# ConvNeXt block and two-layer Mamba mixer in one launch: scan states kept in pairs, multiplied by C in place by GpSimd

## The chip, the core and the metric

The kernel runs on one core of a Trainium2 chip. The metric is device time in microseconds of one execution. The engines are called as in the profile: PE (TensorE, matmuls), PEld (its weight loads), DVE (VectorE), ACT (ScalarE), POOL (GpSimd) and SP (the engine that here only issues DMAs). Each executes its own queue in order and waits on semaphores of the others.

## The reference, cut to what matters

The input is x, 32 images of 96 channels of 56x56 in float32. Layer 0 is a ConvNeXt block, layer 1 two Mamba blocks, a pooled branch, a 1x1 fusion, a batch norm and a residual.

```python
# layer 0
h = depthwise_conv7x7(x) + conv_b                    # groups = 96
h = gelu(layernorm_over_channels(h) @ w1 + b1) @ w2 + b2
x = h * layer_scale + x
# layer 1: seq is x as (image, 3136 positions, 96); two blocks
xz = layernorm(seq) @ in_w                           # 96 -> 2 * 192
xs, z = split(xz)
xc = silu(causal_conv4(xs) + conv_b)
dbl = xc @ xproj_w                                   # 192 -> 6 + 16 + 16
delta = softplus(dbl[:6] @ dt_w + dt_b)
dA  = exp(delta[..., None] * A)                      # 192 channels x 16 states
dBx = delta[..., None] * B[:, None, :] * xc[..., None]
h[t] = dA[t] * h[t-1] + dBx[t]                       # along 3136 positions
y = (sum over states of h * C) + D * xc
seq = seq + (y * silu(z)) @ out_w
# then: fusion with a pooled vector, batch norm, + x
```

The recurrence over h, with 192 x 16 = 3072 rows of 3136 positions for each image and block, is the bulk of the work.

## The kernel before

**Tiling.** The positions of an image are cut into four chunks of CH = 784, each of two halves of HC = 392. A *stage* is one chunk of one image in one Mamba block: 32 x 4 x 2 = 256 stages, one after another, with the two blocks interleaved (line 852). In a stage the 3072 rows are 24 *steps* of 128 partitions: step r is block of 32 channels j = r // 4 (six of them) and state group g = r % 4 (four states for each of the 32 channels, so 128 rows). Each step is one scan of 128x784 on DVE.

**One step.** ACT computes dA with an exponential (`exps`, line 890) from delta spread over the partitions (tile `d4`, by DMA). For blocks j = 0, 1, 3, 4 the factor u = delta * xc is spread to 128 partitions by PE (`spread`, line 905) into a PSUM tile and DVE multiplies it by B (`times_b`, line 878), four times for each block. For blocks 2 and 5 (`POOLED`) POOL does that product in SBUF (`pooled`, line 915). DVE scans (line 938) into a ring of four tiles `h`; one operand is in PSUM, the other in SBUF (`in_psum` tells which). POOL multiplies h by C into a tile `da` (line 942). PE sums the four states of a channel with a 0/1 matrix (`add_up`, line 975, two matmuls of 32 output rows for each step, one for each half) into the PSUM tile `y` of two blocks, which begins with D * xc (line 969). DVE multiplies y by silu(z) (`gate`, line 956), three times in a stage. ACT keeps the last column of h as the start of the next chunk (`keep_state`, line 949), not in the last chunk of an image.

**PSUM.** Eight banks: three for projections (`ps0` to `ps2`), two wide tiles of two banks (`wide(0)` holds the spread u and some exponentials, `wide(1)` products and some exponentials), one for `y`.

**What sets the order.** Every engine's order is written out by hand (`manual_schedule`, line 1011). The loop at line 1021 goes over the steps: in each it emits the exponentials of one or two steps ahead, `keep_state` of the step before, the step's scan with its products, then the spread of the next block and the sums of the step LAG = 3 before. Everything else is cut into *pieces* with a slot, a number in steps relative to a stage: the projections and norms that prepare the next stage (`prep`, 24 steps ahead), the output projection of the last one (`post`), and, in the shade of these, the ConvNeXt block of the later images (`block0`) and the depthwise convolution of the last 20 images (`conv`, five images at a time, one channel pair in each of 192 stages, line 552: seven matmuls of 112x168 and seven of 112x112). A piece with slot 7.5 is emitted behind step 7.

**Buffers.** A tile name has a fixed number of buffers; the writer of a new tile waits until the last reader of an old one is done. Here `da` has 11, `h` 4 (the ring), `bc` (B and C of one group, 6272 bytes a partition) 8, `d4` 3, `u` 1.

Ahead of the stages lie the convolution of the first 12 images and the ConvNeXt block of the first; behind them a normalisation of the whole output from DRAM (lines 1069 to 1078).

Of the kernel before, what the change touches and what calls it, by code (L numbers as in the profile page):

```python
# [44 lines left out]
C = 96  # L45
# [16 lines left out]
def convnext_mamba_kernel(  # L62
# [211 lines left out]
    for i in range(2):  # L274
        d = {}
        lg, lb = column(ln_g[i], C, f"lg{i}"), column(ln_b[i], C, f"lb{i}")
        wz = const.tile([C + 1, 2 * DIN], F32, name=f"inw{i}", tag=f"inw{i}")
        norm_weights(wz, in_w[i], lg, lb)
        wx = const.tile([C + 1, 4, DIN], F32, name=f"wx{i}", tag=f"wx{i}")
        nc.gpsimd.dma_start(wx, taps[i].partition_broadcast(C + 1))  # L280
        for k in range(4):
            nc.vector.tensor_tensor(wx[:, k, :], wx[:, k, :], wz[:, 0:DIN], ALU.mult)
        d["wx"], d["wz"] = wx, wz[:, DIN : 2 * DIN]
# [60 lines left out]
    with ExitStack() as main:  # L344
# [7 lines left out]
        def work(shape, name, bufs):  # L352

            pool, n = (pre[0], 3) if pre else (wp, bufs)
            return pool.tile(shape, F32, name=name, tag=name, bufs=n)
# [42 lines left out]
        xins = {}  # L398

        def block0(b, c, s):  # L400
# [16 lines left out]
            def load_x():  # L417
                if s == 0:
                    xins[b, c] = work([C, CH], "xin", 1)
                    nc.sync.dma_start(xins[b, c], x[b, :, c * CH : (c + 1) * CH])  # L420
# [36 lines left out]
            def down():  # L457
                v["ps"] = psum(2)
                nc.tensor.matmul(
                    v["ps"][0:C, 0:HC], eye, xins[b, c][:, tok(s)], start=True, stop=False  # L460
# [7 lines left out]
            def residual():  # L468
                xs = xins[b, c][:, tok(s)]
                nc.scalar.activation(  # L470
                    xs, v["ps"][0:C, 0:HC], AF.Identity, bias=b2ls,
                    accum_out=batch_sums[b][:, k : k + 1],
                )
                if s == 1:
                    nc.sync.dma_start(x1_d[b][:, c * CH : (c + 1) * CH], xins.pop((b, c)))
# [6 lines left out]
            def pool():  # L482
                ps = psum(2)
# [4 lines left out]
            def fuse():  # L488
                ps = psum(2)
# [9 lines left out]
            last = [(21.5, total), (29.9, pool), (30.9, fuse)] if k == 2 * NCH - 1 else []  # L499
            return last + [  # L500
                (-6, load), (2, load_x), (11.3, center), (12.1, square), (12.4, mean),
                (12.8, root), (14.1, True, norm), (15.6, up), (15.9, gelu), (17.3, down),
                (18.3, residual),
# [28 lines left out]
        PARTS = (0, (NB + 1) // 2), ((NB + 1) // 2, NB)  # L532

        def conv(g, p):
# [11 lines left out]
            def tap(part, dw):  # L546
                first, last = PARTS[part]

                def piece():
                    if dw == 0:  # L550
                        v["ps"] = psum(2)
                    nc.tensor.matmul(  # L552
                        v["ps"][0:R2, 0 : (last - first) * W], v["band"][:, dw, :],
                        xpad[:, first:last, dw : dw + W], start=(dw == 0), stop=(dw == 6),
# [4 lines left out]
            def store(part):  # L559
                first, last = PARTS[part]  # L560
                n = (last - first) * W

                def piece():
                    t = wp.tile([R2, HC], F32, name="sq", tag="sq", bufs=3)
                    nc.scalar.activation(
                        t[:, 0:n], v["ps"][0:R2, 0:n], AF.Identity, bias=cb[:, p : p + 1]
                    )
                    nc.sync.dma_start(
                        conv_d[g][p * R2 : (p + 1) * R2, first * W : last * W], t[:, 0:n]
                    )  # L570

                return piece

            at = (7.7, 8.2, 8.6, 9.2, 9.6, 10.2, 10.4), (18.5, 18.6, 19.2, 20.2, 21.2, 21.3, 22.2)
            return [
                (-1, load), (11.05, store(0)), (22.9, store(1)),
                *[(at[part][dw], tap(part, dw)) for part in range(2) for dw in range(7)],
            ]


        POOLED = (2, 5)
        seqs = {}
# [4 lines left out]
        def prep(S):  # L587
# [28 lines left out]
            def norm():  # L616
                hn = v["hn"] = hns[i]
                if c == 0:
                    nc.vector.memset(hn[:, 0:3], 0.0)
# [88 lines left out]
            def product(lo, hi):  # L708
                def piece():
                    if lo == 0:  # L710
                        S.u = wp.tile([128, NQ, HC], F32, name="u", tag="u", bufs=1)
# [426 lines left out]
```

## Time and profile before

| what | value |
|---|---|
| median of 3 runs | 16957.93 us (16953.4 to 16958.45) |
| the profiled execution | 16951.94 us |
| its span, first to last instruction | 16950.2 us |
| busy: PE / DVE / ACT / POOL | 15327.0 / 15667.8 / 11444.5 / 15657.7 us |
| first POOL product of the stages' steady run | about 570 us after the start |
| last matmul | before 16600 us |

An engine is busy in the profile while at least one of its instructions runs. Instructions of an engine overlap a little at their ends, so the sum of durations is above the busy time, and a stretch of back-to-back instructions tells the cost of one better than its duration does. Matmul ends are modelled: a busy PE is not a PE at its limit. A wait is put down to the instruction that released it last.

### The profile page before, as it was taken

How to read it: one execution, taken by the hardware profiler on the slowest of the kernel's cores; microseconds unless marked ns; L12 is line 12 of the kernel's file. 1: busy time of each engine (PE TensorE's matmuls, PEld its weight loads, DVE VectorE, ACT ScalarE, POOL GpSimd, SP SyncE). 2: the span in 40 equal slices, each digit the busy share in tenths (PEclk: the TensorE clock that was granted, in tenths of full speed). 3: DMA queues.
4: the chain of work that ended last, by engine and by line, in shares of the span. 5: the costliest groups of instructions: out<-in, count | busy, mean ns of one | idle time of the engine just before them, and what ended most of it. 6: DMA issues, size and time to landing. Idle time of an engine off the chain costs nothing. (4 is left out here: it accounts for less than half of the span.)

```text
span 16950.2 us, 206740 instructions
## 1 busy us (share of the span) xinstructions
PE 15327.0 (90%) x69336; PEld 5507.9 (32%) x69336; DVE 15667.8 (92%) x12351; ACT 11444.5 (68%) x18723; POOL 15657.7 (92%) x8798
## 2 busy tenths in 40 slices
PE   8899999999999999999999999999998888888881
PEld 5333333333333333333333333333332222222220
DVE  8699999999999999999999999999999999999994
ACT  1577777777777777777777777677776777676653
POOL 1699999999999999999999999999999999999991
PEclk9899999999999999999999999999999999999985
DMA  4344444444444444444444444444443433433338
GB/s 113 109 139 142 142 135 140 139 142 141 135 142 140 142 135 140 142 141 137 138 141 141 142 134 141 140 143 137 137 142 131 133 126 129 134 132 133 125 121 280
DMA packets 1303109, 2362.11 MB, mean 139 GB/s; under 512 B 516398, under 2 KB 669242, under 8 KB 1302040
## 3 DMA queue, kind: packets, MB, share of 16 engines
q1 hardware_dynamic: 1292712, 2308.46, 42.0%
q10 hardware_dynamic: 7168, 38.54, 0.6%
q8 instruction: 546, 8.95, 0.2%
q14 instruction: 523, 4.28, 0.1%
q0 software_dynamic: 2160, 1.88, 0.1%
HBM read 1945.97 MB, written 402.41 MB: 139 GB/s over the span
## 5 line engine op out<-in xcount | busy, mean ns | idle before, releaser
L942 POOL TENSOR_TENSOR da<-h,bc 128x784 f32<-128x784 f32 x6144 | 11296.0, 1864 | 428.7 <-DVE h L938 356.3
L975 PE MATMUL y<-da,ssum 128*32 128x392 f32 x24576 | 5193.2, 547 | 232.7 <-POOL da L942 229.1
L890 ACT ACTIVATE w<-d,A 128x784 f32<-128x784 f32 x3072 | 2810.9, 916 | 2442.6 <-DVE h L938 2403.6
L938 DVE TENSOR_TENSOR_SCAN h<-w,st,da 128x784 f32<-128x784 f32 x2304 | 4120.7, 1831 | 267.6 <-ACT w L890 261.5
L938 DVE TENSOR_TENSOR_SCAN h<-da,st,w 128x784 f32<-128x784 f32 x2304 | 4176.3, 1834 | 3.6 <-ACT st L949 3.2
L915 POOL TENSOR_TENSOR da<-us,bc 128x784 f32<-128x784 f32 x2048 | 3811.8, 1861 | 0.0
L878 DVE TENSOR_TENSOR w<-w,bc 128x784 f32<-128x784 f32 x3072 | 2910.6, 978 | 325.6 <-PE w L905 257.4
L890 ACT ACTIVATE da<-d,A 128x784 f32<-128x784 f32 x3072 | 2834.6, 939 | 19.0 <-DMA d<-dd 16.0
L633 PE MATMUL ps<-hn,wx 97*64 97x392 f32 x12288 | 2263.2, 503 | 11.0 <-DVE hn L621 11.0
L975 PEld LDWEIGHTS y<-da,ssum 128*32 128x32 f32 x24576 | 1079.4, 116 | 3366.9 <-issue 2015.7
L905 PE MATMUL w<-u,sel 64*128 64x392 f32 x4096 | 992.4, 560 | 555.8 <-DVE h L938 436.8
L938 DVE TENSOR_TENSOR_SCAN h<-w,da 128x784 f32<-128x784 f32 x768 | 1327.4, 1771 | 125.6 <-ACT w L890 118.0
L938 DVE TENSOR_TENSOR_SCAN h<-da,w 128x784 f32<-128x784 f32 x768 | 1345.4, 1773 | 0.0
L633 PEld LDWEIGHTS ps<-hn,wx 97*64 97x64 f32 x12288 | 797.5, 136 | 1422.4 <-issue 1113.2
L712 POOL TENSOR_TENSOR u<-dl,xc 128x784 f32<-128x784 f32 (+1 forms) x512 | 736.9, 1439 | 471.0 <-ACT dl L698 471.0
L552 PE MATMUL ps<-xpad,band 112*112 112x168 f32 (+1 forms) x5376 | 1086.6, 312 | 0.0
L552 PEld LDWEIGHTS ps<-xpad,band 112*112 112x112 f32 x5376 | 709.8, 175 | 1088.3 <-issue 972.7
L690 PE MATMUL ps<-dbl,dtw 6*64 6x392 f32 x3072 | 728.0, 536 | 310.9 <-ACT dbl L668 310.9
L878 DVE TENSOR_TENSOR da<-w,bc 128x784 f32<-128x784 f32 x1024 | 988.0, 965 | 1.0 <-DMA bc<-bd 1.0
L368 ACT ACT_TABLE_LOAD x759 | 973.8, 1283 | 14.2 <-PEq L1125 0.8
L377 ACT ACTIVATE sq<-ps 96x392 f32<-96x392 f32 x768 | 345.1, 490 | 759.9 <-PE ps L372 343.6
L969 PE MATMUL y<-xc,D 128*128 128x392 f32 x1536 | 790.3, 601 | 32.8 <-DVE z L956 32.8
(152 smaller groups left out, 14579.4 us busy)
## 6 DMA issues: line engine op xcount, KB each, us to landing
bc<-bd SPq DMA_DIRECT2D x2048, 392.0 KB, 6.5
d<-dd SPq DMA_DIRECT2D x1536, 392.0 KB, 3.6
us<-uu SPq DMA_DIRECT2D x512, 392.0 KB, 3.3
dd<-dl SPq DMA_DIRECT2D x512, 294.0 KB, 3.7
band<-band_d SPq DMA_DIRECT2D x192, 343.0 KB, 4.3
uu<-u SPq DMA_DIRECT2D x1024, 49.0 KB, 3.0
cv<-conv_d SPq DMA_DIRECT2D x256, 147.0 KB, 3.4
xin<-in_x SPq DMA_DIRECT2D x128, 294.0 KB, 3.9
```

Source lines behind the costliest of these rows:

```text
L368: nc.scalar.preload_act_table_set("natural_log_exp_and_others")
L552: nc.tensor.matmul(v["ps"][0:R2, 0 : (last - first) * W], v["band"][:, dw, :], xpad[:, first:last, dw : dw + W], start=(dw == 0), stop=(dw ...
L633: nc.tensor.matmul(v["x", q][rows(a), 0:HC], weights[:, k, 64 * q : 64 * q + 64], v["hn"][:, o : o + HC], start=(k == 0), stop=(k == last),)
L712: nc.gpsimd.tensor_tensor(S.u[:, lo:hi], v["dl"][:, lo:hi], S.xc[:, lo:hi], ALU.mult)
L878: nc.vector.tensor_tensor(halves(out), S.u4.rearrange("p (a b) -> p a b", a=2)[:, :, 0:HC], halves(S.bcs[g][:, 0, :]), ALU.mult,)
L890: nc.scalar.activation(e, S.d4[j], AF.Exp, scale=S.d["A"][:, j, g : g + 1])
L905: nc.tensor.matmul(S.u4[:, 512 * a : 512 * a + HC], sel[rows(a), j % 2, :], S.u[rows(a), j // 2, :], start=True, stop=True,)
L915: nc.gpsimd.tensor_tensor(product_tile(S, j, g), S.us[j], S.bcs[g][:, 0, :], ALU.mult)
L938: nc.vector.tensor_tensor_scan(ring[:, g, :], S.e.pop((j, g)), db, 0.0 if c == 0 else d["st"][:, j, g : g + 1], ALU.mult, ALU.add,)
L942: nc.gpsimd.tensor_tensor(da, ring[:, g, :], S.bcs[g][:, 1, :], ALU.mult)
L969: nc.tensor.matmul(S.y[:, 0:HC], S.d["D"][:, q, :], S.xc[:, q, :], start=True, stop=False)
L975: nc.tensor.matmul(S.y[r0 : r0 + 32, 0:HC], ssum, da[:, tok(a)], start=False, stop=(g == NG - 1),)
```

## The change

All of it is in the stages and their preparation.

1. **State pairs.** The scans of g = 0, 1 and of g = 2, 3 write the two halves of one SBUF tile `h` of 128 x 2 x 784 (7 buffers; `states`). The ring and the role of `da` as product tile go; `da` (now 4 buffers, NE) holds exponentials alone. The product of u and B of g = 3, and the pooled products, are written into the `h` tile, and the scan runs in place over them.
2. **h*C in place.** POOL multiplies a whole pair by C in one instruction of 128 x 2 x 784, in place. Where a next chunk follows, the instruction leaves out the last column (2 x 783); `keep_state` copies that column and multiplies it by C with two ACTIVATEs of 128x1.
3. **Pooled products** also go in pairs (two instructions for a block, with u broadcast over the pair), emitted at the slots in `AHEAD`, and **u** is one POOL instruction for all three q (128x1176) at slot 13.8, not one of 784 and one of 392.
4. **B and C** lie in tiles of their own, `bp` (3 buffers) and `cp` (4), each for two groups; the eight loads of a stage remain and two move to slots 15 and 17.9.
5. **State sums.** `add_up` takes the pairs of both blocks of a `y` at once, eight matmuls in a row to the four column tiles 0, 32, 64, 96, twice for each y, four steps behind.
6. **Spreads and gates** get fixed steps: spreads of blocks 0, 3 and 4 are emitted one step earlier than before (SPREADS), gates at steps 5, 13 and 20.
7. **Depthwise convolution in one part:** seven matmuls of 112x280 at steps 4 to 10, one store; none at steps 18 to 22.
8. **Slots** of the preparation are set anew; the input of the ConvNeXt block is loaded, and its result stored, by half chunks; half of the in_w weights is copied to a tile of its own and the other half freed after setup.

```diff
-            at = (7.7, 8.2, 8.6, 9.2, 9.6, 10.2, 10.4), (18.5, 18.6, 19.2, 20.2, 21.2, 21.3, 22.2)
+            at = (4.9, 6.1, 7.2, 8.6, 9.2, 9.6, 10.4)
+            return [(-1, load), (10.5, store), *[(at[dw], tap(dw)) for dw in range(7)]]
...
+        AHEAD = {(2, 0): -0.1, (2, 1): 4.4, (5, 0): 12.1, (5, 1): 16.9}
...
-            t = (-7.6, -7.5, -6.5, -6, 0, 0.1, 1, 2.3, 3.1, 3.4, 4)
+            t = (-4.5, -4.4, -5.3, -2.9, -4.2, -0.3, 0.8, 2.3, 2.9, 3.4, 4)
...
-        ring = wp.tile([128, NG, CH], F32, name="h", tag="h", bufs=1)
-        LAG = 3
-        LATE = (4, 12)
+        NE = 4
+        LAG = 4
+        LAG0 = 4
+        GATES = (5, 13, 20)
+        SPREADS = [(22, 0), (27, 1), (34, 3), (38, 4)]
+        WS = ((0, 3), (1, 2), (), ())
...
+        def states(S, j, h):
+            if (j, h) not in S.h:
+                S.h[j, h] = wp.tile([128, 2, CH], F32, name="h", tag="h", bufs=7)
+            return S.h[j, h]
...
-                nc.gpsimd.tensor_tensor(
-                    product_tile(S, j, g), S.us[j], S.bcs[g][:, 0, :], ALU.mult
-                )
+                nc.gpsimd.tensor_tensor(
+                    states(S, j, h), S.us[j].unsqueeze(1).broadcast_to([128, 2, CH]), S.bc[0, h],
+                    ALU.mult,
+                )
...
             nc.vector.tensor_tensor_scan(
-                ring[:, g, :], S.e.pop((j, g)), db, 0.0 if c == 0 else d["st"][:, j, g : g + 1],
-                ALU.mult, ALU.add,
+                h[:, g % 2, :], S.e.pop((j, g)), S.pb.pop((j, g), h[:, g % 2, :]),
+                0.0 if c == 0 else d["st"][:, j, g : g + 1], ALU.mult, ALU.add,
             )
-            nc.gpsimd.tensor_tensor(da, ring[:, g, :], S.bcs[g][:, 1, :], ALU.mult)
+            if g % 2 == 1:
+                hc = h[:, :, 0 : CH if c == NCH - 1 else CH - 1]
+                nc.gpsimd.tensor_tensor(hc, hc, S.bc[1, g // 2][:, :, 0 : hc.shape[2]], ALU.mult)
...
-                nc.scalar.copy(
-                    S.d["st"][:, j, g - 1 : g + 1].unsqueeze(2), ring[:, g - 1 : g + 1, CH - 1 : CH]
-                )
+                h, last = S.h[j, g // 2], slice(CH - 1, CH)
+                nc.scalar.copy(S.d["st"][:, j, g - 1 : g + 1].unsqueeze(2), h[:, :, last])
+                for k in range(2):
+                    nc.scalar.activation(
+                        h[:, k, last], h[:, k, last], AF.Identity,
+                        scale=S.bc[1, g // 2][:, k, last],
+                    )
...
-            for a in range(2):
-                r0 = 64 * a + 32 * (j % 2)
-                nc.tensor.matmul(
-                    S.y[r0 : r0 + 32, 0:HC], ssum, da[:, tok(a)],
-                    start=False, stop=(g == NG - 1),
-                )
+            hs = [S.h.pop((2 * q + k, half)) for k in range(2)]
+            for g in range(2):
+                for k in range(2):
+                    for a in range(2):
+                        r0 = 64 * a + 32 * k
+                        nc.tensor.matmul(
+                            S.y[r0 : r0 + 32, 0:HC], ssum, hs[k][:, g, tok(a)],
+                            start=False, stop=(half == 1 and g == 1),
+                        )
...
-                    if n % NG == NG - 1:
-                        spread(n + 1)
+                    for k, j in SPREADS:
+                        if n >= k - NSTEP and (n - k) % NSTEP == 0:
+                            spread(((n - k) // NSTEP + 1, j))
```

## The prediction

> **What bounds the kernel now.** I read the busy table first, then two stretches of the stages, then the waits, then single instructions. A measurement of this kernel can tell about 0.2%, 34 us, from no change.
>
> ```profile
> PE 15327.0 (90%) x69336; PEld 5507.9 (32%) x69336; DVE 15667.8 (92%) x12351; ACT 11444.5 (68%) x18723; POOL 15657.7 (92%) x8798
> ```
>
> Three engines seem equally full, so the whole span does not decide. The stretch 4000 to 12000 us has convolution pieces in every stage, 13000 to 16000 us none (the 192 pairs are used up). Columns: busy us and instructions of PE, PEld, DVE, ACT, POOL, then clock, DMA share and GB/s.
>
> ```profile
> 4000.00:12000.00 8000.00, 7541.04 (x34841) 2709.31 (x34839) 7587.62 (x5928) 5653.24 (x9335) 7801.02 (x4348) 0.96 0.43 140
> 13000.00:16000.00 3000.00, 2680.03 (x11776) 888.54 (x11773) 2853.86 (x2234) 2102.03 (x3417) 2934.66 (x1638) 0.93 0.40 130
> ```
>
> The scan line has 3070 instructions in the first and 1156 in the second. At 24 for each stage a stage takes 8000 x 24 / 3070 = 62.54 us with and 62.28 us without convolution. Per stage POOL is busy 60.98 us (60.92 without), DVE 59.32, ACT 44.2. POOL is 97.5% and 97.8% busy: it is the bound, DVE 1.7 us behind. DVE's waits in the two stretches, and the same for the second:
>
> ```profile
> DVE h L938 <- ACT w L890: 197.8, 135, 1.7
> DVE w L878 <- PE w L905: 151.0, 183, 1.1
> DVE z L956 <- PE y L975: 23.0, 44, 1.5
> ```
>
> ```profile
> DVE h L938 <- ACT w L890: 60.5, 49, 2.4
> DVE z L956 <- PE y L975: 58.2, 35, 4.0
> ```
>
> With convolution the waits are 2.9 us a stage, for exponentials and for the spread; without it the spread is never late, yet DVE waits 2.7 us, now for y, whose sums wait for POOL. The time stayed and only the name of the wait moved: DVE is held to POOL's pace. That is why I count POOL's instructions first.
>
> ```profile
> L942 POOL TENSOR_TENSOR da<-h,bc 128x784 f32<-128x784 f32 x6144 | 11296.0, 1864 | 428.7 <-DVE h L938 356.3 <-DVE hn L619 24.7 <-PE y L975 19.2
> L712 POOL TENSOR_TENSOR u<-dl,xc 128x784 f32<-128x784 f32 x256 | 473.8, 1851 | 471.0 <-ACT dl L698 471.0
> L712 POOL TENSOR_TENSOR u<-dl,xc 128x392 f32<-128x392 f32 x256 | 263.2, 1028 | 0.0
> ```
>
> ```profile
> 8013.76 10.94 POOL L942 TENSOR_TENSOR da<-h,bc 128x784 f32<-128x784 f32 x6
> ...
> 8028.31 1.02 POOL L712 TENSOR_TENSOR u<-dl,xc 128x392 f32<-128x392 f32 x1
> 8029.29 1.85 POOL L942 TENSOR_TENSOR da<-h,bc 128x784 f32<-128x784 f32 x1
> ```
>
> Here the reader sees what one POOL instruction costs in a row: six of 784 in 10.94 us, 1.82 each; one of 392 is followed after 0.98. So 2.14 ns for an element and 0.14 us for an instruction. From the durations (1851 and 1028) it is 2.10 ns and 0.205 us.
>
> And DVE's two regular waits of a stage, at its first product (step 0) and its fourth scan (step 3):
>
> ```profile
> 8018.26 0.98 DVE L878 TENSOR_TENSOR w<-w,bc 128x784 f32<-128x784 f32 x1 [0.78 <-PE w L905]
> ...
> 8028.70 1.79 DVE L938 TENSOR_TENSOR_SCAN h<-w,da 128x784 f32<-128x784 f32 x1 [1.63 <-ACT w L890]
> ```
>
> **What the Trainium skill says.** "GPSIMD Engine Reference", § 3.1 Elementwise: a two-input tensor_tensor of 2048 fp32 takes 4497 ns. My two numbers give 0.14 + 2048 x 2.14 = 4.52 us, so the line through 392 and 784 carries on to the 1568 elements of a pair, which no trace shows yet. "SBUF — State Buffer", § Who interferes with whom: a DVE instruction with two SBUF inputs blocks against a POOL instruction that reads SBUF, one with a single SBUF input does not. The trace agrees as far as it goes: scans with one operand in PSUM take 1831 and 1834 ns in the two arrangements while POOL is 97% busy. After the change each product and scan still has one of each, so I charge no contention. "TensorEngine Tiling (Array Packing)", § Key Properties: tiles of the array work in parallel; the sums now use two column tiles in turn (four matmuls in 0.85 us), after the change four.
>
> **The change, part by part, for a stage.**
>
> POOL. 24 products with C and 8 pooled ones become 12 and 4, u two to one: 17 instructions fewer, elements the same (the missing last column is 0.04 us). Saving 17 x 0.14 = 2.4 us by the rhythm, 3.5 us by the durations. I take 2.4: POOL 60.98 - 2.4 = 58.6 us. Unknown is what writing in place, two rows of 783 instead of one of 784, and the broadcast u cost. Ends: 57.5 us (3.5 saved); 61.3 us, if a pair costs 5% more than counted (16 x 0.17 = 2.7). A loss is not excluded.
>
> DVE. The same 24 scans, 16 products, three gates and the norms: 59.3 us. Scanning in place is the nearest to the form with `da` as input (1831 ns): 0. DVE becomes the bound, by 0.7 us.
>
> ACT. `keep_state` gains two ACTIVATEs of 128x1 for each of 12 pairs in three of four stages, 18 on average. The nearest row is the 96x1 negation, 195 ns; "ScalarE: Activation LUTs", § What ACT_TABLE_LOAD costs, has 186 ns plus 93 for a pointer operand, less 93 of overlap. So 18 x 0.19 = 3.4 us (5.0 at 0.28), less 0.25 for one convolution store: 47 to 49 of some 60 us. They hide in ACT's wait for DVE to free a wide tile (2403.6 us in the run, 9.4 a stage). Behind them are the exponentials; in a pooled block DVE takes 1.79 a step and ACT 0.86 for the exponential, 0.19 more a step on average. If that cover is gone, it is 0.4 us for each pair.
>
> PE. 48 sum matmuls in 12 groups of four, 0.85 each: 10.2 us. In six groups of eight, 5 us if four tiles work at once, 9 if not (eight two-tile projections take 1.54). Seven convolution matmuls of 280 columns, about 0.42 (between 331 ns for 168 and 451 for 336 columns, carried on), 2.9 us for 4.4. PE is not the bound; what counts is its order. The spread of block 0 stood behind convolution taps at 8015.55 and 8016.91 and started at 17.29; block 5's third scan had freed the tile at about 8015.7. It now comes a step earlier, without taps in front: the 0.8 us wait goes, and the like before block 3. The scan's wait at step 3 comes from ACT, which stood 1.58 us behind the convolution store at slot 22.9 (now 10.5) and 1.08 us for the third projection (slot 0.1, now -0.3). What is late next is POOL itself, or DVE has nothing to wait for.
>
> SP. Eight loads of B and C as before; four loads and four stores of half chunks more for an image, one convolution store less a stage. The load at slot 17.9 waits for DVE to leave `bp` at step 17; behind it are u's store and `d4`. The us tile is needed at step 23, some 15 us later, the two transfers take 3.0 + 3.3: 0. The smaller tiles at the start: 0, within 10 us.
>
> Latency. POOL starts a product only when two scans are done. The tightest sum, that of block 1 at PE step 9 behind scan 5, has 3 x 1.79 = 5.4 us for 3.5: hidden while POOL lags under 1.9 us.
>
> **The sum.** A bound engine in this coupling idles 1.56 us a stage with and 1.36 without convolution (62.54 - 60.98, 62.28 - 60.92). With DVE as the bound I take 1.4: 59.3 + 1.4 = 60.7 us. Saved 192 x 1.84 + 64 x 1.58 = 454 us. From the profiled execution, 16951.9 (its span of 16950.2 and 1.7 around it): 16497. The median stands 6 us higher: 16503, rounded 16500. The 957 us outside the stages are left as they are.
>
> **Rivals**, priced as 256 stages from a mean of 62.5 us.
> - *Nearly full DVE.* The two regular waits go and nothing follows: 59.5 to 60.1 us, 16196 to 16350. For it: both waits have named causes that are moved. Against: POOL has only 0.7 us to spare.
> - *POOL stays the bound*, since in-place pairs save less than counted or nothing: 59.9 to 60.9 busy plus 1.4, 61.3 to 62.3 us, 16657 to 16913, middle 16785. For it: the form is unseen. Against: the line of 392, 784 and 2048.
> - *Nothing gained*: DVE's waits are ACT's and PE's own, and stay near 3 us: 16924 to 16992. Against: the moving name of the wait above.
> - *Slower: seven `h` tiles.* At slot 16.9 POOL's product for block 5 needs an eighth tile; one comes free only when PE reads the pairs of blocks 2 and 3 at step 17, behind the ConvNeXt matmuls of slot 15.6. The product of slot 4.4 likewise hangs on the sums of step 3, behind the z projections. POOL waits in order, with the next products by C, so the sums and y, behind it. At 58.6 us busy it can lose 3.9 us a stage before a stage is as long as now, so it decides from about 2 us at each place; with 2.5, 63.6 us a stage, 17240. For it: PE already stands behind such work (520.6 us for dbl in the run). Against: PE gets freer.
>
> **Chances.** Forecast (60.1 to 61.3 us, 16350 to 16657) 0.50; nearly full DVE 0.16; POOL still the bound 0.18; nothing gained 0.04; slower 0.12. Range 16250 to 16880: it leaves out the slower and the equal case and 0.02 at each end. Faster 0.50 + 0.16 + 0.18 = 0.84, same 0.04, slower 0.12.
>
> **What would show it.** POOL pairs near 3.5 us and u near 2.65; POOL's busy time a stage under DVE's, which stays at 59.3; no wait of the first product for the spread; scans at 1.83. It is wrong if pairs take 3.65 or more, if POOL waits for PE at the pooled products, or if DVE's waits stay near 3 us a stage.

## The result, and the profile after

| | before | after |
|---|---|---|
| median | 16958.19 us (16953.4 to 16967.83, 4 runs) | 16698.44 us (16695.08 to 16705.25, 4 runs) |
| ratio, 95% interval | | 0.9847 (0.983 to 0.9864) |
| profiled span | 16950.2 us | 16693.4 us |
| mean granted TensorE clock | 0.943 | 0.871 |

The kernel became 1.5% faster, by 260 us; 458 us were forecast (16500). The time lies in the range given (16250 to 16880), but outside the band of the forecast itself (16350 to 16657). The busy table of the kernel after:

```profile
PE 13702.7 (82%) x66648; PEld 5300.0 (32%) x66648; DVE 15622.8 (94%) x12353; ACT 12429.3 (74%) x23139; POOL 15025.8 (90%) x4446
```

The groups of the changed instructions (pairs by C, pooled pairs, u, the last column):

```profile
L932 POOL TENSOR_TENSOR h<-h,cp 128x1566 f32<-128x1566 f32 (+1 forms) x3072 | 10753.6, 3523 | 408.2 <-DVE h L926 394.5
...
L909 POOL TENSOR_TENSOR h<-us,bp 128x1568 f32<-128x1568 f32 x1024 | 3608.9, 3524 | 265.8 <-PE y L975 161.7
...
L697 POOL TENSOR_TENSOR u<-dl,xc 128x1176 f32<-128x1176 f32 x256 | 684.3, 2673 | 598.2 <-ACT dl L685 469.8
...
L942 ACT ACTIVATE h<-h,cp 128x1 f32<-128x1 f32 x4608 | 1105.6, 287 | 102.1 <-ACT st L940 1.5
```

Every POOL duration is the forecast one: 3.52 us for a pair (3.5), 2.67 for u (2.65). The two stretches of the stages, after (columns as in the prediction):

```profile
4000.00:12000.00 8000.00, 6805.72 (x33497) 2632.73 (x33499) 7657.49 (x6003) 6215.57 (x11627) 7578.84 (x2202) 0.88 0.45 141
13000.00:16000.00 3000.00, 2445.55 (x12042) 881.02 (x12042) 2915.55 (x2290) 2341.71 (x4400) 2885.24 (x839) 0.87 0.42 134
```

They hold 3108 and 1182 scans, so a stage takes 8000 x 24 / 3108 = 61.78 us with convolution and 60.91 without; 60.7 was forecast for both. In the first stretch (129.5 stages) POOL is busy 58.5 us a stage, DVE 59.1, ACT 48.0: again the forecast numbers. What is not as forecast is DVE's idle time: 61.78 - 59.13 = 2.65 us a stage, and 1.7 without convolution, where the sum had 1.4. DVE's waits, first stretch and then second:

```profile
DVE h L926 <- ACT w L884: 275.5, 174, 3.6
...
DVE z L950 <- PE y L975: 0.3, 1, 0.3
```

```profile
DVE h L926 <- ACT w L884: 57.3, 52, 2.3
```

No wait for a spread is left and none for y; all that counts is one kind, scans that wait for an exponential. Adding up DVE's idle pieces over 0.1 us by the step that follows (stages 40 to 169 with convolution, 200 to 249 without, counted from 0) shows which scans. Stage lengths in this table are from the starts of the scans in the same stages:

| us a stage, with convolution | before | after |
|---|---|---|
| step 0, spread from PE | 0.79 | - |
| step 3, exponential from ACT | 1.47 | - |
| step 10, exponential | - | 0.50 |
| step 12, spread | 0.38 | - |
| step 19, exponential | - | 1.59 |
| step 20, y | 0.17 | - |
| all idle pieces | 3.03 | 2.46 |
| stage | 62.55 | 61.80 |
| *without convolution:* all idle pieces / stage | 2.83 / 62.35 | 1.49 / 60.82 |

The three waits that the prediction named are gone, and a new one at step 19 is larger than any of them. It is 0.85 us in stages without convolution, where the kernel before waited 1.20 us at step 3 and 1.26 at step 20. One instance in full, DVE first:

```profile
8085.94 3.57 DVE L926 TENSOR_TENSOR_SCAN h<-da,st,w 128x784 f32<-128x784 f32 x2
8091.54 1.85 DVE L926 TENSOR_TENSOR_SCAN h<-w,st,h 128x784 f32<-128x784 f32 x1 [2.03 <-ACT w L884]
```

The exponential that it waits for, on ACT:

```profile
8087.91 0.19 ACT L808 ACTIVATION_READ_ACCUMULATOR sq<-seq,neg 96x1 f32 x1
8090.02 0.58 ACT L469 ACTIVATE xin<-ps,b2ls 96x392 f32<-96x392 f32 x1 [1.92 <-PE ps L463]
8090.51 0.19 ACT L469 ACTIVATION_READ_ACCUMULATOR xin<-ps,b2ls 96x1 f32 x1
8090.60 0.90 ACT L884 ACTIVATE w<-d,A 128x784 f32<-128x784 f32 x1
```

ACT sat 1.92 us ready to compute the exponential, behind line 469 in its order: `residual`, the last step of the ConvNeXt block, which waited for matmuls. The change moved it from slot 18.3 to 17.6, that is, to ahead of this exponential. Why the matmuls were late, on PE (the trace shows each matmul of the program as two instructions, and the counts are of instructions):

```profile
8077.88 1.68 PE L899 MATMUL w<-u,sel 64*128 64x392 f32 x4 [3.49 <-DVE h L926]
8079.49 4.29 PE L443 MATMUL ps<-hz,w_sb 97*128 97x392 f32 x6
8083.57 1.51 PE L967 MATMUL y<-xc,D 128*128 128x392 f32 x2
8085.01 2.17 PE L975 MATMUL y<-h,ssum 128*32 128x392 f32 x16
8087.11 0.90 PE L459 MATMUL ps<-xin,eye 96*96 96x392 f32 x2
8087.85 2.14 PE L463 MATMUL ps<-gl,w_sb 128*96 128x392 f32 x6
```

PE stood 3.49 us before the spread of block 4 (step 14), the wide tile of which DVE had not yet freed. Then six instructions of line 443 (`up`, the first projection of the ConvNeXt block) took 4.29 us; those of line 463 (`down`, the second one), of as many columns, six in 2.14. The granted clock in these pieces of the same stage (third column from the end):

```profile
8078.00:8084.00 6.00, 6.00 (x11) 2.90 (x12) 5.89 (x6) 3.83 (x7) 5.47 (x3) 0.50 0.22 74
8084.00:8090.00 6.00, 6.00 (x28) 1.86 (x28) 5.48 (x5) 4.01 (x9) 4.42 (x2) 0.80 0.00 1
8090.00:8094.00 4.00, 4.00 (x32) 1.43 (x34) 2.36 (x3) 3.85 (x11) 4.00 (x2) 1.00 0.50 140
```

PE ran at half its clock from within the pause to 8086.4 us. So the chain of this stage is: PE pauses, comes back at half clock, `down` ends late, `residual` waits on ACT, the exponential stands behind it, DVE waits. How much of the wait the clock makes is a question of its own. Counted from the start of the scan of step 14, `down` ended 13.1 us later before the change and 13.6 us later after it (means of the 130 stages), so it is late by only some 0.5 us more than it was; the larger difference is what now stands behind it.

The Trainium skill, "TensorE: Matmul & The Clock Gate", Part 1, says that the array falls to half its clock after an idle window of about 3.4 us, with no values between. The two values agree with this trace (its clock records say 0.50 or 1.00; the 0.80 above is a mean over a change). The pause does not: in 4000 to 12000 us the clock was halved around 127 of the 128 pauses of 2.5 to 4.4 us ahead of block 4's spread, but also around 95 pauses of 2.1 us ahead of convolution taps. Before the change PE has no pause of 2.5 us in that stretch, and its clock was still halved 129 times, though never in the matmuls of line 443.

### The profile page after: what moved, and what is told of

Read it like the earlier page. It is cut to its first block, busy times and chain, and to the rows that moved or that the text cites. A ratio compares the mean times of both kernels' runs of the same rounds, so it can differ in the third digit from the quotient of the medians.

```text
span 16693.4 us, 199266 instructions
## 1 busy us (share of the span) xinstructions
PE 13702.7 (82%) x66648; PEld 5300.0 (32%) x66648; DVE 15622.8 (94%) x12353; ACT 12429.3 (74%) x23139; POOL 15025.8 (90%) x4446
## 5 line engine op out<-in xcount | busy, mean ns | idle before, releaser
L932 POOL TENSOR_TENSOR h<-h,cp 128x1566 f32<-128x1566 f32 (+1 forms) x3072 | 10753.6, 3523 | 408.2 <-DVE h L926 394.5
L926 DVE TENSOR_TENSOR_SCAN h<-w,st,h 128x784 f32<-128x784 f32 x2304 | 4106.7, 1828 | 316.9 <-ACT w L884 311.2
L926 DVE TENSOR_TENSOR_SCAN h<-da,st,w 128x784 f32<-128x784 f32 x2304 | 4172.4, 1831 | 0.5 <-ACT da L884 0.5
L909 POOL TENSOR_TENSOR h<-us,bp 128x1568 f32<-128x1568 f32 x1024 | 3608.9, 3524 | 265.8 <-PE y L975 161.7
L871 DVE TENSOR_TENSOR w<-w,bp 128x784 f32<-128x784 f32 x3072 | 2908.5, 977 | 144.3 <-PE w L899 19.6
L975 PE MATMUL y<-h,ssum 128*32 128x392 f32 x24576 | 2547.4, 525 | 65.6 <-POOL h L932 65.4
L926 DVE TENSOR_TENSOR_SCAN h<-w,h 128x784 f32<-128x784 f32 x768 | 1324.8, 1769 | 162.9 <-ACT w L884 162.7
L546 PE MATMUL ps<-xpad,band 112*112 112x280 f32 x2688 | 1051.6, 515 | 337.0 <-ACT dl L685 337.0
L942 ACT ACTIVATE h<-h,cp 128x1 f32<-128x1 f32 x4608 | 1105.6, 287 | 102.1 <-ACT st L940 1.5
L443 PE MATMUL ps<-hz,w_sb 97*128 97x392 f32 x1536 | 1055.3, 858 | 0.4 <-DVE hz L438 0.4
L871 DVE TENSOR_TENSOR h<-w,bp 128x784 f32<-128x784 f32 x1024 | 987.1, 964 | 0.0
```

The costliest lines, as they stand in the source:

```text
L443: nc.tensor.matmul(v["pss"][f][:, 0:HC], w1_sb[:, f * 128 : (f + 1) * 128], hn0s[s], start=True, stop=True,)
L546: nc.tensor.matmul(v["ps"][0:R2, 0 : NB * W], v["band"][:, dw, :], xpad[:, :, dw : dw + W], start=(dw == 0), stop=(dw == 6),)
L871: nc.vector.tensor_tensor(halves(S.pb[j, g]), S.u4[j].rearrange("p (a b) -> p a b", a=2)[:, :, 0:HC], halves(S.bc[0, g // 2][:, g % 2, :]) ...
L909: nc.gpsimd.tensor_tensor(states(S, j, h), S.us[j].unsqueeze(1).broadcast_to([128, 2, CH]), S.bc[0, h], ALU.mult,)
L926: nc.vector.tensor_tensor_scan(h[:, g % 2, :], S.e.pop((j, g)), S.pb.pop((j, g), h[:, g % 2, :]), 0.0 if c == 0 else d["st"][:, j, g : g + ...
L932: nc.gpsimd.tensor_tensor(hc, hc, S.bc[1, g // 2][:, :, 0 : hc.shape[2]], ALU.mult)
```

## The experiments

Theory, formed from the traces: DVE's time is its own 59 us and the places where it waits for work queued in order on ACT and PE; the missing part of the gain is at step 19. Rivals: POOL sets the pace, so its saving is what gained and its rest is what is missing; or the slower PE does. Each expectation stands as it was written ahead of its run, with theories of its own. The times of numbers 1, 2, 3, 6, 7 and 9 came out in the range of neither theory. Ratios are to the kernel before.

**1. `residual` back at its old slot**

```diff
-                (17.6, residual),
+                (18.3, residual),
```

> The changed kernel with one slot set back: the residual of the ConvNeXt block (ACT, waits for PE) at 18.3 as before the change, not at 17.6, so that ACT issues the exponential of step 19 ahead of it. In the changed kernel DVE waits 1.59 us a stage at step 19 for that exponential. Theory A, ACT's order is the cause: the wait at step 19 falls under 0.3 us, a stage goes from 61.8 to 60.3 to 60.9 us, time 16350 to 16480. Theory B, DVE is held by POOL and the wait only changes its name: the wait at step 19 goes, another comes at another step, time within 60 us of 16698.

Measured: 16602.5 us, 0.9786 (0.9771 to 0.9801); stages of 61.14 and 60.58 us. DVE's waits, 4000 to 12000 us:

```profile
DVE z L950 <- PE y L975: 108.5, 103, 2.1
DVE h L926 <- ACT w L884: 86.6, 42, 3.4
```

The wait at step 19 is gone. Half of it came back one step on: the third gate, at step 20, now finds y not ready (0.76 us a stage). So the place of `residual` in ACT's order is shown to make the step-19 wait, and the next wait behind it is found.

**2. The fusion copies later**

```diff
-            pieces = [(7.9, project), (8.9, move(0)), (9.9, move(1))]
+            pieces = [(7.9, project), (10.2, move(0)), (10.3, move(1))]
```

> The changed kernel with the two copies of the output projection (ACT, wait for PE) at slots 10.2 and 10.3, behind the exponential of step 11, not at 8.9 and 9.9. In the changed kernel DVE waits 0.50 us a stage at step 10, in single stages 3.6 us. Theory A, ACT's order: that wait goes, 0.3 to 0.5 us a stage, time 16570 to 16640. Theory B, DVE is held by POOL: within 30 us of 16698.

Measured: 16959.45 us, 1.0 (0.9991 to 1.0008).

```profile
DVE hz L438 <- ACT ps L391: 203.1, 120, 3.4
DVE h L926 <- ACT w L884: 163.5, 134, 2.3
DVE w L871 <- PE w L899: 74.4, 46, 2.7
```

The wait at step 10 went (0.50 to nothing), but two new ones came: the ConvNeXt norm at step 14 waits 1.66 us a stage for ACT, and the spread at step 12 is late by 0.56. Their place fits the PSUM banks, which the copies now empty later and the next projection needs; that link is read from the order, not tried. The whole gain of the change can be lost by moving two copies of 0.6 us.

**3. Sums with two column tiles in turn instead of four**

```diff
-            for g in range(2):
-                for k in range(2):
+            for k in range(2):
+                for g in range(2):
```

> The changed kernel with the sums of a y in the order block, group, half, so that two column tiles alternate and not four; the same matmuls. Theory A: four tiles at once save PE some 5 us a stage, PE stands idle longer in one piece and its clock is lowered (0.87 against 0.94 before); with two tiles the sums take about 1.4 us for eight matmuls and not 0.76, the clock rises to 0.90 or more, other matmuls get shorter, ACT waits less for PE, time falls by 50 to 200 us. Theory B: the clock has nothing to do with it; PE only loses time, DVE's waits stay or grow, time 16698 to 16900.

Measured: 16678.4 us, 0.9831 (0.9815 to 0.9848), so no loss. The sums' group in this kernel:

```profile
L975 PE MATMUL y<-h,ssum 128*32 128x392 f32 x12448 | 1260.8, 516 | 0.1
```

and in the kernel after:

```profile
L975 PE MATMUL y<-h,ssum 128*32 128x392 f32 x12440 | 1242.0, 514 | 6.6 <-POOL h L932 6.6
```

Before the change:

```profile
L975 PE MATMUL y<-da,ssum 128*32 128x392 f32 x12276 | 2592.1, 543 | 42.3 <-POOL da L942 42.2
```

That is 20.3 us a stage before and 9.6 after. The edit changed the order in the program, but it did not take the four tiles apart: by the starts in the trace, four sum instructions still begin within 33 ns and the next four 330 ns after the first, as in the kernel after (within 20 ns, and 330), while before the change two begin within 7 ns and the next two after 353. So the halving is that of four tiles at work and not two. Whether this has to do with the granted clock, 0.871 in both kernels, was therefore not tested.

**4. Each POOL pair in two instructions again**

```diff
-                nc.gpsimd.tensor_tensor(hc, hc, S.bc[1, g // 2][:, :, 0 : hc.shape[2]], ALU.mult)
+                for k in range(2):
+                    nc.gpsimd.tensor_tensor(
+                        hc[:, k], hc[:, k], S.bc[1, g // 2][:, k, 0 : hc.shape[2]], ALU.mult
+                    )
```

and the pooled pairs likewise: 16 POOL instructions more a stage.

> The changed kernel with every pair product of POOL in two instructions of 784 or 783 columns, in place as before; u stays one. 16 instructions more a stage. If the gain of the change is POOL's fixed cost, POOL is busy 58.5 + 16 x 0.14 = 60.8 us a stage and becomes the bound again: a stage of 62.2 to 62.9 us, time 16800 to 16980. If the gain comes from the order of the other engines and POOL's load does not matter, time stays within 50 us of 16698.

Measured: 16727.84 us, 0.9863 (0.9848 to 0.9878).

```profile
4000.00:12000.00 8000.00, 6790.72 (x33409) 2651.79 (x33407) 7648.62 (x5998) 6207.84 (x11621) 7840.67 (x4269) 0.88 0.45 141
```

POOL is busy 7840.67 of 8000 us, as full as before the change, and about 29 us of 260 are lost, less than the 34 us that the prediction calls measurable. The waits at steps 10 and 19 stay (0.58, 1.57). In this kernel POOL's saving is not what gained.

**5. The kernel before, with less work for POOL**

```diff
-            nc.gpsimd.tensor_tensor(da, ring[:, g, :], S.bcs[g][:, 1, :], ALU.mult)
+            nc.gpsimd.tensor_tensor(
+                halves(da)[:, :, 0:358], halves(ring[:, g, :])[:, :, 0:358],
+                halves(S.bcs[g][:, 1, :])[:, :, 0:358], ALU.mult,
+            )
...
-                    S.y[r0 : r0 + 32, 0:HC], ssum, da[:, tok(a)],
+                    S.y[r0 : r0 + 32, 0:358], ssum, da[:, a * HC : a * HC + 358],
```

The products with C and the sums leave out the last 34 columns of each half, so PE has less to do as well as POOL.

> The kernel before, with less work for POOL: the product with C and the sums over states leave out the last 34 columns of each half, so y lacks the scan's part there. POOL's 24 products take 716 columns for 784, 3.5 us a stage less: about 57.5 us busy; DVE's work is the same, PE's sums are 9% shorter. Theory A, POOL was the bound of the kernel before: a stage falls from 62.5 to 60.5 to 61.2 us, time 16450 to 16630. Theory B, the order of ACT and PE held DVE and POOL's load did not matter (as splitting POOL's pairs in the changed kernel cost only 30 us): a stage stays at 62.0 to 62.5, time 16830 to 16960.

Measured: 16842.52 us, 0.9929 (0.9915 to 0.9944); stages of 62.28 and 61.76 us.

```profile
4000.00:12000.00 8000.00, 7509.83 (x34992) 2758.98 (x34988) 7602.90 (x5953) 5677.64 (x9373) 7420.84 (x4366) 0.95 0.44 140
```

```profile
DVE z L959 <- PE y L978: 128.3, 46, 4.1
DVE h L938 <- ACT w L890: 120.3, 129, 1.2
DVE w L878 <- PE w L905: 101.8, 167, 1.0
```

POOL has some 3.2 us a stage less to do and falls from 97.5% to 92.8% busy; a stage is 0.27 us shorter with convolution and 0.6 without. But this mean hides two kinds of stage. The spacing of line 443's instructions tells whether PE was at half clock there (653 ns) or not (329):

| 130 stages with convolution | stages | us a stage | idle | step 20, y |
|---|---|---|---|---|
| before, line 443 at full clock | 130 | 62.55 | 3.03 | 0.17 |
| number 5, at full clock | 99 | 61.37 | 2.09 | 0.19 |
| number 5, at half clock | 31 | 65.19 | 5.56 | 3.53 |

PE, with shorter sums, now pauses for up to 3.0 us (2.5 before), and in a quarter of the stages it is at half clock behind block 4's spread and y is late. In the other stages 1.2 us of the 3.2 are gained. So the small gain of the mean does not show that POOL's load counted for nothing in the kernel before. Nor do the 1.2 us show that it did, since PE's sums got shorter too. What PE waited for POOL ahead of its sums in 4000 to 12000 us, before and in this run:

```profile
PE y L975 <- POOL da L942: 42.2, 126, 1.1
```

```profile
PE y L978 <- POOL da L942: 1.0, 1, 1.0
```

**6. The kernel before, with the new order of convolution and spreads alone**

```diff
-        PARTS = (0, (NB + 1) // 2), ((NB + 1) // 2, NB)
+        PARTS = ((0, NB),)
...
-                    if n % NG == NG - 1:
-                        spread(n + 1)
+                    ahead = {22: 2, 3: 1, 10: 2, 14: 2}.get(n % NSTEP)
+                    if ahead:
+                        spread(n + ahead)
```

with the taps and the store at the slots of the new kernel, and the pooled vector of the ConvNeXt block in other PSUM banks.

> The kernel before, with the order of PE alone changed as in the new one: depthwise convolution in one part (taps at 4.9 to 10.4, store at 10.5, pooled vector in the other PSUM banks), spreads of blocks 0, 3, 4 one step earlier. POOL's instructions are those of before. Theory A, POOL was the bound: DVE's waits at steps 0, 3 and 12 (2.6 us a stage) go but come back elsewhere, a stage near the 62.3 us of the stretch without convolution, time 16870 to 16960. Theory B, order: the waits stay gone, a stage of 60.8 to 61.8 us, time 16550 to 16800. If the earlier spreads leave PE idle over 2.5 us in one piece before block 4's, its matmuls behind take double, as in the changed kernel.

Measured: 17405.14 us, 1.0259 (1.0242 to 1.0276); stages of 64.85 and 62.82 us.

```profile
DVE z L956 <- PE y L975: 358.0, 204, 3.4
DVE h L938 <- ACT w L890: 266.3, 199, 2.3
```

```profile
PE w L905 <- DVE h L938: 391.0, 215, 2.4
```

The spreads are never late now, and yet a stage is 2.3 us longer: y is late at steps 12 (1.59 us) and 20 (1.34). The wait at step 3 stays at 1.21 us, although the convolution store has left slot 22.9. The early spreads of blocks 0 and 4 wait on PE for their tile (391.0 us, before 167.7), and the sums, only three steps behind here, stand after them. At step 12 the sums stand behind larger taps and the spread without a pause of PE; that link is read from the order. In 64 of the 130 stages line 443 is at half clock, and these take 66.38 us (y late at step 20 by 2.34); the other 66 take 63.37 (0.37), still longer than before. So this part of the change alone does not give the gain. Whether it would with the later sums and gates (LAG 4, steps 5, 13, 20) that came with the pairs was not run.

**7. Matmuls in PE's pause**: the D term of the second y, three times over the same values, at step 14 ahead of the spread and no longer at step 17, behind line 443

```diff
+                    if n % NSTEP == 14:
+                        begin(stages[n // NSTEP], 1)
                     for k, j in SPREADS:
```

> The changed kernel, with the D term of the second y emitted at step 14 ahead of block 4's spread and not at step 17, three times over (the last one counts, the result is the same). It breaks the idle stretch of PE ahead of that spread, 2.5 to 4.2 us in the changed kernel, up to 2.4 in the one before. In the traces the next ConvNeXt matmuls start 654 ns apart behind stretches of 2.5 us and more, 329 ns behind shorter ones. Theory A, the idle stretch halves PE's clock and this makes ACT and so DVE late: spacing back to 329 ns, clock above 0.90, the wait at step 19 falls from 1.59 to under 0.8 us a stage, time 16450 to 16600. Theory B, the clock does not follow the idle stretch or the wait not the clock: spacing 654 ns or the wait at 1.3 to 1.6 us, time 16650 to 16750.

Measured: 16630.61 us, 0.9803 (0.9789 to 0.9818). The matmuls of line 443 in this kernel, in the kernel after, and before:

```profile
L443 PE MATMUL ps<-hz,w_sb 97*128 97x392 f32 x780 | 361.3, 610 | 0.0
```

```profile
L443 PE MATMUL ps<-hz,w_sb 97*128 97x392 f32 x777 | 548.5, 878 | 0.0
```

```profile
L443 PE MATMUL ps<-hz,w_sb 97*128 97x392 f32 x762 | 285.4, 511 | 0.0
```

With the pause filled most of the slowing of line 443 is gone (83 of 130 stages are at full clock there), and the wait at step 19 falls from 1.59 to 0.05 us a stage. This does not show that the half clock made the wait: in the 47 stages that are still at half clock it is 0.14 us, so that the D term no longer stands ahead of `down` is nearly enough. The clock does lengthen the way: from the start of line 443 to the end of `down` it is 8.65 us in these 47 stages and 6.58 in the 83 (10.02 in the kernel after). How the 1.59 us divide between the two stays open. The pauses have moved, too. None of 2.5 us is left ahead of block 4's spread, but 84 stand ahead of block 0's, where there was none. The mean clock is only 0.878, and an exponential at step 3 is now late by 1.26 us, so a stage still takes 61.45.

**8. `residual` at 18.3 and the third gate of a stage, that of its second y, a step later**

```diff
-                (17.6, residual),
+                (18.3, residual),
...
-        GATES = (5, 13, 20)
+        GATES = (5, 13, 21)
```

> The changed kernel with the residual at 18.3, and the second gate at step 21, not 20. With the residual alone set back, the wait of step 19 went (1.59 us) and 0.76 us a stage came up at step 20, where the gate waits for y. Theory A, order: with the gate a step later this wait goes too, a stage of 60.2 to 60.6 us, time 16340 to 16460. Theory B, POOL (58.5 us busy) now holds the rest: the wait moves on, a stage near 61.1, time 16540 to 16610.

Measured: **16393.29 us** (16391.4 to 16398.06), 0.9663 (0.9649 to 0.9678): the fastest of the kernels that compute everything.

```profile
4000.00:12000.00 8000.00, 6967.63 (x34272) 2723.20 (x34271) 7826.49 (x6141) 6362.10 (x11947) 7743.91 (x2252) 0.88 0.47 144
```

```profile
DVE h L926 <- ACT w L884: 106.8, 115, 2.5
```

A stage takes 8000 x 24 / 3179 = 60.40 us (60.17 without convolution). No arithmetic differs from the kernel after, and 305 us are gained by two numbers in the order. Line 443 still takes 864 ns here and the mean clock is 0.866, so this time is reached with the half clock; what it still costs here was not tried.

**9. Number 8 with number 4's split POOL instructions**

> The kernel residual_gate (changed kernel, residual at 18.3, second gate at 21; 60.4 us a stage, 16393 us) with every pair product of POOL in two instructions, 16 more a stage; POOL about 60.6 us busy. Theory A, POOL's fixed cost matters as soon as nothing else holds the stage: POOL becomes the bound again, a stage of 61.6 to 62.3 us, time 16690 to 16880. Theory B, POOL's load never decides: 16390 to 16440.

Measured: 16538.13 us, 0.975 (0.9735 to 0.9764).

```profile
4000.00:12000.00 8000.00, 7010.48 (x33870) 2760.23 (x33871) 7753.29 (x6079) 6287.53 (x11786) 7941.20 (x4326) 0.87 0.46 143
```

```profile
DVE h L926 <- ACT w L884: 167.6, 181, 2.8
DVE h L926 <- POOL h L933: 12.7, 11, 1.2
```

Now the same 16 instructions cost 145 us in place of 29, and POOL is busy 99.3%, 60.6 us of a stage of 61.05. That is more than the whole stage of number 8 takes, so with the order mended POOL is the bound, as it was not in the kernel after. DVE's waits don't show it: only 12.7 us of them are put down to POOL.

**10. Number 8 without the two ACTIVATEs on the last column**

```diff
-                for k in range(2):
-                    nc.scalar.activation(
-                        h[:, k, last], h[:, k, last], AF.Identity,
-                        scale=S.bc[1, g // 2][:, k, last],
-                    )
```

> The kernel residual_gate without the two ACTIVATEs that multiply the last column of a pair by C: that column's sums over states are left unmultiplied. ACT has 18 small instructions a stage less, about 4.3 us by their records (287 ns each). Theory A, ACT's added work is part of what is left of DVE's waits (0.8 us a stage for exponentials at steps 10 and 20): waits fall below 0.5 us, 30 to 120 us faster, 16270 to 16360. Theory B, it hides in ACT's waits: within 25 us of 16393.

Measured: 16346.0 us, 0.9637 (0.9622 to 0.9651). The last column of a pair is left without its factor C, so the kernel computes less.

```profile
DVE h L926 <- POOL h L932: 41.5, 43, 1.7
DVE h L926 <- ACT w L884: 36.9, 78, 1.8
```

Taking 1105.6 / 256 = 4.3 us of ACT's work a stage away gives about 47 us, 0.18 us a stage: some 4% of it was not hidden. The largest wait left, at step 10, is now for POOL (0.32 us a stage).

**11. Number 8 with the fusion projection a step earlier**

```diff
-            pieces = [(7.9, project), (8.9, move(0)), (9.9, move(1))]
+            pieces = [(6.9, project), (8.9, move(0)), (9.9, move(1))]
```

> The kernel residual_gate with the output projection (PE) at slot 6.9, not 7.9, ahead of the convolution taps of 7.2. ACT's copies at 8.9 and 9.9 wait for it, and DVE at step 10 behind them (0.46 us a stage). Theory A, PE's order: that wait falls under 0.2 us, a stage of 60.0 to 60.2, 16290 to 16350. Theory B, the projection is late because PE runs at half clock there, whatever its slot: within 40 us of 16393, or slower where it stands ahead of sums.

Measured: 16425.19 us, 0.9682 (0.9666 to 0.9698); the wait at step 10 stays at 0.48 us a stage. The copies there do wait for these matmuls, but an earlier place in PE's order does not make them ready earlier: counted from the scan of step 7 the projection starts 0.41 us earlier than in number 8 and ends 0.07 us earlier. What would mend step 10 stays open.

**12. The kernel after with its spreads back a step**

```diff
-        SPREADS = [(22, 0), (27, 1), (34, 3), (38, 4)]
+        SPREADS = [(23, 0), (27, 1), (35, 3), (39, 4)]
```

> The changed kernel with the spreads of blocks 0, 3 and 4 one step later, where they stood before the change (steps 23, 11, 15); POOL's pairs, the sums, the gates and the convolution in one part stay. Theory A, the spreads' place is where the change gains: DVE's waits for the spread at steps 0 and 12 come back, 1.0 to 1.3 us a stage, and since splitting POOL's pairs cost 30 us and the two-tile order of the sums nothing, they are about all of the gain: 16880 to 17020. Theory B, the taps that stood in front of the spreads were the cause and are gone: no wait for the spread, time 16600 to 16750. Should the idle stretch of PE ahead of block 4's spread fall under 2.5 us, the ConvNeXt matmuls behind it start 329 ns apart, not 654, and the wait at step 19 falls.

Measured: 16714.22 us, 0.9852 (0.9836 to 0.9869).

```profile
DVE h L926 <- ACT w L884: 271.8, 162, 2.7
DVE w L871 <- PE w L899: 6.6, 18, 0.4
```

The spreads are still in time (0.05 us a stage), so the earlier step is not what ended the waits of steps 0 and 12. At step 0 the taps are gone that stood directly in front of the spread in all 130 stages before. At step 12 taps stand directly in front here too, and yet PE has 0.38 us to wait for the tile; the sums between the taps take half their time now, but what made PE early enough there was not isolated.

The stages of all of them, with and without convolution, and DVE's idle pieces by step (with convolution):

| kernel | stage | without | idle, us a stage | the largest |
|---|---|---|---|---|
| before | 62.55 | 62.35 | 3.03 | step 3 ACT 1.47, step 0 PE 0.79 |
| 5 before, less POOL | 62.28 | 61.76 | 2.91 | step 20 y 0.99, step 3 ACT 0.93 |
| 6 before, new order | 64.85 | 62.82 | 5.20 | step 12 y 1.59, step 20 y 1.34 |
| after | 61.80 | 60.82 | 2.46 | step 19 ACT 1.59, step 10 ACT 0.50 |
| 1 residual | 61.14 | 60.58 | 1.85 | step 20 y 0.76, step 10 ACT 0.63 |
| 2 copies | 63.17 | 60.90 | 3.76 | step 14 ACT 1.66, step 19 ACT 1.22 |
| 3 two tiles | 61.70 | 61.01 | 2.35 | step 19 ACT 1.52 |
| 4 POOL split | 61.84 | 61.08 | 2.49 | step 19 ACT 1.57 |
| 7 PE kept busy | 61.45 | 60.87 | 2.20 | step 3 ACT 1.26 |
| 12 late spreads | 61.82 | 60.80 | 2.48 | step 19 ACT 1.75 |
| 8 residual, gate | 60.40 | 60.17 | 1.13 | step 10 ACT 0.46 |
| 9 the same, POOL split | 61.05 | 60.63 | 1.71 | step 10 ACT 0.76 |
| 10 the same, no last column | 60.27 | 59.77 | 0.98 | step 10 POOL 0.32 |
| 11 the same, projection | 60.58 | 60.18 | 1.31 | step 10 ACT 0.48 |

In every row a stage is 59.2 to 59.7 us and the idle pieces: DVE's work never changed, and all that moved is where it waits.

## Why the prediction was right in part

**Right.** The sizes of the new work: POOL's pair 3.52 us (3.5 forecast), its busy time 58.5 us a stage (58.6), DVE 59.1 (59.3), ACT 48.0 (47 to 49). The last column's ACTIVATE takes 287 ns, the upper end given (0.28). The line of POOL's price carried on from 784 to 1568 elements. Scans in place take 1828 ns and the others 1831, so nothing was to be added. The waits at steps 0 and 3 went as said, and the one before block 3 too. For step 0 number 12 leaves the taps in front as the half of the named cause that counts. For step 3 the named store cannot be the main cause: without convolution, where there is no such store, the kernel before waited 1.20 us there, and number 6, with the store at slot 10.5, 1.21; the moved projection, the other thing named, was not tried alone. y is never late (0.3 us in 8000), so the later start of POOL's products is hidden. The seven `h` tiles cost 161.7 us of POOL's time in the run at the pooled products, 0.6 us a stage, under the 2 us from which that rival decides.

**Not borne out: "POOL is the bound", "DVE is held to POOL's pace".** The reason was that the wait changed its name and the time stayed. In the new kernel it does not hold: number 4 makes POOL as full as ever and costs about 29 us of 260. So the first half of the sum (2.4 us saved on POOL, hence the gain) had the wrong cause; the gain came with the waits at steps 0, 3 and 12, listed as by-products. For the old kernel it stays open how far POOL held DVE. Without convolution (13000 to 16000 us) the sums did wait for POOL, as the prediction says:

```profile
PE y L975 <- POOL da L942: 107.2, 108, 2.7
```

and in number 5 the stages at full clock gained 1.2 us of 3.2, with less work for POOL and PE together. With convolution the two largest waits ended at ACT and PE, so the rival "nothing gained" was nearer to them ("ACT's and PE's own"), with the wrong guess of where they would end.

**Wrong by a factor of two: PE's sums.** The prediction took every matmul instruction of the trace for a matmul, but there are two to each. The sums took 20.3 us a stage before, not 10.2, and the convolution taps 5.7, not 4.4. The 9.6 us of sums measured after agree with its "9 if not" (four tiles not at once) by luck: they are what four tiles at once take (number 3).

**Wrong: the term "I take 1.4".** An idle time taken over from the old bound has no reason to hold for another engine and another order: it was 2.65 us with convolution and 1.7 without. The excess, (61.78 - 60.7) x 192 + (60.91 - 60.7) x 64 = 221 us, is the whole shortfall of 198 and a little more. Most of it sits at step 19, since number 1 removes that wait with one slot. And that slot was in the diff: `residual` went from 18.3 to 17.6, past an exponential. The prediction passed over "slots of the preparation are set anew" apart from two pieces that came earlier, and priced none that moved in front of an exponential. It also took for granted that a freer PE is a faster one; its mean clock fell from 0.943 to 0.871, which lengthens the way to the end of `down` (number 7), by how much of the 1.59 us is open.

That the forecast stage of 60.7 us was within reach, number 8 shows: 60.40. The measured 16698 lies outside the forecast's own band and in that of the rival "POOL stays the bound" (16657 to 16913), but not by that rival's mechanism, since the pairs cost no more than counted. That the range held was partly luck: it was wide enough because it took in a rival that did not come true.

**Open.** No one part carries the step from 62.5 to 61.8 us: the order alone in the old kernel loses (number 6), and pairs with the old order were not run. Why PE now pauses longer before block 4's spread was not isolated. Its sums take half the time and stand in groups of eight every four steps; the taps take about what they took (5.7 us a stage before, 5.5 after).

## What to carry to other kernels

A nearly full engine is not yet the bound: give it a little less or a little more to do and see whether the time follows (here 29 us in one order, 145 in a better one, for the same 16 instructions). Look then at whether the trial changed something else: number 5 also slowed PE in a quarter of the stages, and the mean over all of them hid a gain in the rest. Where several engines are about 95% full and each runs in a fixed order, price every moved slot by what is queued behind it on its own engine while it waits, ACT's above all, since its exponentials feed the scans. After a wait is removed, look for the next instruction that was only just in time.

## What the runs showed of the hardware

- Line 443's instructions of 392 columns start 653 ns apart at a granted clock of 0.50 and 329 ns apart at 1.00. No one length of a pause decides which: behind pauses of up to 2.46 us ahead of block 4's spread they were always at 329 ns in the kernel before, but in number 6, where PE never pauses longer, at 653 ns in 64 of 130 stages.
- In 4000 to 12000 us the kernel after has 247 stretches at half clock. Each lasts 3.41 us or a whole multiple (3.41 us 69 times, 6.83 43 times, 10.24 134 times, 17.07 once), and they start on one grid of that step. The 129 of the kernel before are of 3.41 and 6.83 us.
- The clock can stay low although PE is nearly full. The longest of these stretches, in the kernel after:

```profile
8048.00:8062.00 14.00, 13.31 (x34) 5.45 (x34) 12.70 (x10) 8.24 (x15) 13.59 (x5) 0.50 0.36 94
```

  PE is busy 13.31 of 14 us, at half clock throughout. More often, after a pause ahead of block 4's spread, full clock came back 7.7 us after PE had gone on (median of 127). The page cited above has it come back after some 3.4 us of steady work; these do not agree, and no run here says why.
- Sums of 32 output rows start four at a time on four column tiles (within 20 ns, the next four 330 ns later) and two at a time on two (within 7 ns, the next two after 353).
- POOL can be busy 99.3% of a long stretch (number 9), in one order of the instructions, while DVE is 97% busy beside it.
- One ACTIVATE of 128x1 with its scale from SBUF takes 287 ns; the 96x1 one with an immediate took 195.
